# Three layers in one kernel: activations transposed in 32 x 32 squares on VectorE and through memory, side work metered by VectorE columns, float32 products in larger groups

## Chip, core and metric

The kernel runs on one core of a Trainium2 chip. The metric is device time in microseconds (us); shown are the median and the spread of three runs. The profile is of one further execution, taken by the hardware profiler. Four engines compute: TensorE (PE; its loads of stationary operands are listed apart as PEld), VectorE (DVE), ScalarE (ACT) and GpSimd (POOL). SyncE (SP), ACT and POOL can each start DMA transfers from a queue of their own.

## The reference

The input x has 4 sequences of 1024 rows with 256 channels. Three layers follow, each added to its input:

```python
def ffn(x):                      # applied to layernorm(x), times 0.5
    h = silu(x @ w1.T * s1) * (x @ w2.T * s2)     # 256 -> 1024
    h = gelu(h @ h1.T * t1)                       # 1024 -> 1024
    h = gelu(h @ h2.T * t2)                       # 1024 -> 1024
    return h @ w3.T * s3                          # 1024 -> 256
def mix(x):                      # applied to layernorm(x)
    K = kernel taps of length 1024 for each channel, from exp, sin and cos of parameters
    y = irfft(rfft(x, 2048) * rfft(K, 2048))[:1024]     # along the sequence
    return gelu(y) @ W.T + b
x = x + 0.5 * ffn(layernorm(x)); x = x + mix(layernorm(x)); x = x + 0.5 * ffn(layernorm(x))
```

The weights of `ffn` are whole numbers -1, 0 and 1, and all arithmetic has to be good to float32.

## The kernel before

**Blocks.** The 4096 rows are cut into 8 blocks of 512. The first feed-forward layer is done for blocks f0 to f7, then the last for g0 to g7, one after another by `ffn` (L275). Between them lies `mix` (L698), once for each sequence (two blocks); it needs both f blocks of its sequence and has to be stored before the first g block of that sequence is read.

**A block.** The feed-forward products have the channels on the partitions and the 512 rows as the moving columns. Activations are kept in two parts, the value rounded to a shorter float (fp32r) and what is left of it, so each product is done twice with the same weights (`linear`, L263, matmul on L267). Layer 1 makes `pa` and `pb` for eight m; layers 2 and 3 make one `p` for each of eight m, 16 matmuls each. After each `p`, ACT does the gelu (L299) and the rounding (L301), and DVE subtracts to get the low part (`low_part`, L240). At the end `result` multiplies the last activations, now the stationary side, with `w3_sb` (matmul `po`, L323), 64 matmuls; for each half of these, `finish` scales on DVE, adds the block's input on POOL and stores.

**Next block's input.** `prepare` (L834) is a generator that is advanced by `ahead()`. Before, `ahead()` is called after each of the eight m of layer 3 and once more with `last=True`. It loads the next block's 512 rows, normalises them (`norm`, L208: statistics on DVE, square root on ACT, two-operand scaling on DVE) and, at `last=True`, calls `transposed` (L242): eight TensorE transposes of 128 x 128 into two PSUM banks (L248), from which DVE makes the rounded and the low part. Rows lie on partitions as `positions` says: partition p holds rows 8p to 8p+7 of its sequence, and a block is one half of these eight.

**Side work.** `tick()` (L871) advances `all_aside` (L856) by one step, 15 times for each block: after each m of layers 2 and 3 but the last of each, and once after `ahead(last=True)`. `all_aside` first computes the kernel's taps (`kernel_steps`, L501), their transform (`kernel_spectrum`, L670), then the four `mix`. These use plain float32 matmuls: `pk` (L552), `pf` (L621), `pi` (L791), `pw` (L811). A step is what lies between two `yield`; how much DVE work is in it differs. In `kernel_steps`, each step multiplies one group of eight channels on DVE and issues the `pk` products of the group before. In `spectrum` (L593) each step issues the products of one of four q. After the 60th tick every third also runs a step of `weight_checks` (L362): a copy of the weights is read again and compared on DVE. If the side work is not far enough when a g block wants its rows, `prepare` drains it in a loop.

**Order.** The instructions of each engine are issued in one order, fixed when the kernel is built. It follows the order of the code, but a scheduler may put a later instruction ahead of one that it takes to be not ready. Small tiles of 512 columns (`half`, L132) share 19 slots, the two-part activations (`ring`, L136) 15, the 512-row inputs (`xb`) 3, and PSUM has 8 banks. All loads and stores after the start are on the queue of SP.

Of the kernel before, what the change touches and what calls it, by code (L numbers as in the profile page):

```python
# [17 lines left out]
P = 128  # L18
# [6 lines left out]
JT = TB // P  # L25
N2 = 32
# [6 lines left out]
STEPS = 2 * KH - 1  # L33
# [22 lines left out]
CST_WIDTH = 56  # L56

# [36 lines left out]
def macaron_layers(  # L94
# [32 lines left out]
    tt, ts, stt = nc.vector.tensor_tensor, nc.vector.tensor_scalar, nc.vector.scalar_tensor_tensor  # L127
# [22 lines left out]
    w3_sb = keep.tile([P, KH, D], wide, name="w3_sb")  # L150
# [8 lines left out]

    k_hat = dram.tile([2 + len(PAIRS), 2, P, 2, D], F32, name="k_hat")  # L160
# [6 lines left out]

    def load_x(t, blk, name, queue=nc.sync):
        b, g = divmod(blk, J // JT)
        xb = work.tile([P, JT, D], F32, tag="xb", name=name, bufs=3)  # L170
        queue.dma_start(xb, positions(t, b, g * JT, JT))
        return xb
# [4 lines left out]

    weights_from = nc.gpsimd if split else nc.sync

    x_first = work.tile([P, JT, D], F32, tag="xb", name="x_f0", bufs=3)  # L180
    for i, queue in ((0, nc.sync), (2, nc.scalar)):
        queue.dma_start(x_first[:, i : i + 2, :], positions(x, 0, i))
# [10 lines left out]

    x_second = load_x(x, 1, "x_f1", queue=weights_from)
# [4 lines left out]
    for t, src in ((h1_sb, h1), (h2_sb, h2)):  # L199
        for k in range(0, KH, 2):  # L200
            weights_from.dma_start(t[:, k : k + 2, :], rows(src)[:, k : k + 2, :])
    weights_from.dma_start(w3_sb, rows(w3))
# [5 lines left out]
    def norm(t, name, parts_of=1):  # L208

        stats = small.tile([P, JT, 6], F32, tag="stats", name=f"stats_{name}")  # L210
        mv = small.tile([P, JT, 2], F32, tag="mv", name=f"mv_{name}")
        rstd = small.tile([P, JT], F32, tag="rstd", name=f"rstd_{name}")
        step = JT // parts_of
        for at in range(0, JT, step):
            here = range(at, at + step)
            for i in here:
                nc.vector.bn_stats(stats[:, i, :], t[:, i, :])
            for i in here:
                nc.vector.bn_aggr(mv[:, i, :], stats[:, i, :])
            nc.scalar.activation(  # L220
                rstd[:, at : at + step], mv[:, at : at + step, 1], AF.Sqrt, bias=eps
            )
# [15 lines left out]
    def low_part(t, src):  # L238

        return tt(t[:, 1, :], src, t[:, 0, :].bitcast(F32), ALU.subtract)  # L240

    def transposed(xn, name, first=False):  # L242

# [18 lines left out]

    def linear(ps, w, m, acts):  # L263
# [11 lines left out]
    def ffn(xt, src, dst, blk, name, tick, ahead, final):  # L275

        ha = []
        for m in range(KH):  # L280
# [6 lines left out]
            stt(g if split else t[:, 0, :], pb, sc_sb[:, 1, m : m + 1], g, ALU.mult, ALU.mult)  # L287
# [4 lines left out]
        for layer, w in ((2, h1_sb), (3, h2_sb)):  # L292
            hb = []
            for m in range(KH):
# [9 lines left out]
                if layer == 3:  # L304
                    ahead()
                if m < KH - 1:
                    tick()
            ha = hb
        ahead(last=True)
        tick()  # L310
        b, g = divmod(blk, J // JT)
        rest = []
        for i in range(0, JT, 2):
            xr = half(f"xr_{name}_{i}", 2, D)
            nc.sync.dma_start(xr, positions(src, b, g * JT + i))
            rest.append(xr)
# [14 lines left out]
        def finish(ps, y, xr, i, n, add_on):  # L331
            stt(
# [8 lines left out]
            nc.sync.dma_start(positions(dst, b, g * JT + i, n), y)  # L341
# [20 lines left out]
    def weight_checks():  # L362
# [9 lines left out]
        assert len(todo) == N_CHECKS  # L372
        for n, (src, held) in enumerate(todo):
            given = half(f"given_{n}", *held.shape[1:])
            nc.sync.dma_start(given, src)
# [14 lines left out]
        nc.vector.tensor_reduce(total, miss[:, 0:N_CHECKS], axis=mybir.AxisListType.X, op=ALU.add)  # L390
        ps = psum.tile([1, 1], F32, tag="ps", name="p_bad")
# [109 lines left out]
    def kernel_steps():  # L501
# [7 lines left out]
        for g0 in range(0, DD, group):  # L509
# [34 lines left out]
            def products():  # L544

                nonlocal pk
                for d1, a in ready:
                    at = d1 % per_tile
                    if at == 0:
                        pk = psum.tile([P, per_tile, 2, NB], F32, tag="ps", name=f"pk_{g0 + d1}")  # L550
                    for i in range(n):
                        nc.tensor.matmul(  # L552
                            pk[0:NA, at + i, :, :].rearrange("p h b -> p (h b)"),
                            a[:, i].rearrange("p a b -> p (a b)"),
                            qd[d1 // per_tile][:, at + i, :, :].rearrange("p h b -> p (h b)"),
                            start=True,
                            stop=True,
                        )
                    if at + n == per_tile:
                        first = g0 + d1 + n - per_tile  # L560
                        for i, t in enumerate(taps):
                            for over in range(NB // J):
                                b0 = over * J + 2 * i
                                nc.scalar.copy(
                                    t[over * NA : (over + 1) * NA, :, :, first : first + per_tile],
                                    pk[0:NA, :, :, b0 : b0 + 2].rearrange("p d h b -> p b h d"),
                                )
                ready.clear()

            for d1 in range(0, group, n):  # L570
# [12 lines left out]
                products()  # L583
                ready.append((d1, a))
                yield
            products()
# [6 lines left out]
    def spectrum(rows_of, name, over=1):  # L593
# [39 lines left out]
        m_next = matrix(order[0])  # L633
        yield
        got = {}
        for n, q in enumerate(order):
            m = m_next
            if n + 1 < len(order):
                m_next = matrix(order[n + 1])
            products(q, m)  # L640
            if n:
                sums(order[n - 1])
            if n == 3:
                a0 = add(u[0], u[2], ALU.add, "a0")
                a1 = add(u[0], u[2], ALU.subtract, "a1")
            yield
        sums(order[3])
        b0, b1 = add(u[1], u[3], ALU.add, "b0"), add(u[1], u[3], ALU.subtract, "b1")
        yield
# [20 lines left out]
    def kernel_spectrum():  # L670
# [5 lines left out]
        for got in spectrum(rows_of, "k", over=NB // J):  # L676
            yield
        minus = half("k_minus", 2, D)
        for n, m in enumerate((0, 4)):
            t = got[m]  # L680
            nc.scalar.mul(minus[:, n, :], t[:, 1, :], -1.0)
            for e in range(2):
                nc.sync.dma_start(k_hat[n, 0, :, e], t[:, 0, :])
            nc.sync.dma_start(k_hat[n, 1, :, 0], minus[:, n, :])
            nc.sync.dma_start(k_hat[n, 1, :, 1], t[:, 1, :])
            yield
        for n, (a, b) in enumerate(PAIRS):
# [4 lines left out]
            nc.sync.dma_start(k_hat[n, 0, :, 0], t[:, 0, :])  # L692
            nc.sync.dma_start(k_hat[n, 0, :, 1], o[:, 0, :])
            nc.sync.dma_start(k_hat[n, 1, :, 0], minus[:, 0, :])
            nc.sync.dma_start(k_hat[n, 1, :, 1], t[:, 1, :])
            yield

    def mix(b):  # L698

        xn = [load_x(x1, 2 * b + g, f"xm_{b}_{g}") for g in range(2)]  # L700
        yield
        for g in range(2):
            yield from norm(xn[g], f"m{b}_{g}")
        got = None
        for got in spectrum(lambda j: xn[j // JT][:, j % JT, :], f"m{b}"):
            yield
# [17 lines left out]
        yield  # L724
# [50 lines left out]
        for j in range(JQ):  # L775
# [8 lines left out]
            if j % 2:  # L784
                yield
        banks = [[bank(f"pi_{b}_{dc}_{e}") for e in range(2)] for dc in range(DC)]
# [15 lines left out]
        yield  # L802
        for j in range(0, J, 2):
            xr = half(f"xr_{b}_{j}", 2, D)
            nc.sync.dma_start(xr, positions(x1, b, j))
            if j % 4 == 0:
                yield
            ps = bank(f"pw_{b}_{j}")
            for e in range(2):
                for dc in range(DC):  # L810
                    nc.tensor.matmul(  # L811
                        ps[:, e * D : (e + 1) * D],
                        yts[dc][j // JQ][:, (j % JQ + e) * P : (j % JQ + e + 1) * P],
                        wt_sb[:, dc, :],
                        start=(dc == 0),
                        stop=(dc == DC - 1),
                    )
            y = half(f"yw_{b}_{j}", 2, D)
            tt(
                y,  # L820
                ps.rearrange("p (e d) -> p e d", e=2),
                bias_sb[:, None, :].to_broadcast([P, 2, D]),
                ALU.add,
            )
            nc.gpsimd.tensor_tensor(y, xr, y, ALU.add)
            nc.sync.dma_start(positions(x2, b, j), y)
# [7 lines left out]
    def prepare(turn, blk, upcoming):  # L834

        name = f"{turn}{blk}"
        if turn == "f":
# [3 lines left out]
        else:  # L841
            while ("m", blk // 2) not in done:
                next(aside, None)
            xb = load_x(x2, blk, f"x_{name}")
# [5 lines left out]
        while True:  # L850
            if ("last layer", blk, turn) in done:
                upcoming.extend(transposed(xb, name))
                return
            yield

    def all_aside():  # L856
# [3 lines left out]
        yield from kernel_spectrum()  # L860
        for b in range(B):
            while ("f", 2 * b + 1) not in done:
                yield
            yield from mix(b)
# [4 lines left out]
    ticks = 0  # L869

    def tick():  # L871

        nonlocal ticks
        next(aside, None)
        ticks += 1
        if ticks > 4 * STEPS and ticks % 3 == 0:
            next(checks, None)
# [7 lines left out]
    xt, last_split = transposed(x_first, "f0", first=True)  # L885
    for n, (turn, blk) in enumerate(blocks):
# [92 lines left out]
```

## Time and profile before

| what | value |
|---|---|
| median of three runs (lowest to highest) | 1430.31 us (1430.04 to 1430.56) |
| the profiled execution: its time, its span | 1430.35 us, 1428.6 us |
| DVE busy | 835.0 us (58%) |
| ACT busy | 678.6 us (48%) |
| POOL busy | 81.6 us (6%) |
| DMA: bytes moved, mean rate | 85.50 MB, 60 GB/s |
| matmuls `p` of layers 2 and 3 | 4096, 0.39 us each by their own duration |
| transposes `pt` | 128, 0.27 to 0.29 us each by their own duration |

The span is the time from the first to the last instruction; the device time is a little longer. A matmul's own duration is longer than the distance to the next one, since matmuls are pipelined: what a matmul costs the engine is the distance between starts, not the duration. The chain of waits follows the work that ended last back to the start and gives each piece the time by which it delayed the end, which for a full TensorE comes to the same thing. A wait is listed with the engine that waited, what it waited for, the total, the count and the longest one.

### The profile page before, as it was taken

To read this page: it belongs to the slowest core of one execution; us is meant where nothing else is said; L and a number is where in the kernel's file an instruction comes from. 1 tells how busy PE (TensorE), PEld (TensorE's weight loads), DVE (VectorE), ACT (ScalarE), POOL (GpSimd) and SP (SyncE) were. 2 spreads that over 40 slices of the span, in tenths; PEclk is the share of its full clock that TensorE was granted. 3 is DMA by queue.
4 is the path that set the end of the run, shared out by engine and by line. 5 is a ranking of instruction groups with operands and counts; after the bars stand their busy time and mean duration, and the time that the engine had idled before them with its cause. 6 is when DMAs were issued, how large, how long until landed. Compare 5 with 4: busy or idle time off the path is not lost.

```text
span 1428.6 us, 18125 instructions
## 1 busy us (share of the span) xinstructions
PE 1416.6 (99%) x7092; PEld 1199.8 (84%) x7092; DVE 835.0 (58%) x1584; ACT 678.6 (48%) x1033; POOL 81.6 (6%) x82
## 2 busy tenths in 40 slices
PE   9999999999999999999999999999999999999997
PEld 7888888888888888888888888888888888888886
DVE  6786566753836577562877633867447766341412
ACT  5875468744435435344453433534345344443432
POOL 4010000100000000020000010000010000100000
PEclk9999999999999999999999999999999999999999
DMA  9010000101122140140231130231131301200000
GB/s 372 36 45 0 31 15 1 45 4 44 69 85 67 38 134 21 60 133 16 74 96 51 45 127 15 75 96 38 60 103 59 92 35 41 92 30 1 23 8 18
DMA packets 43278, 85.50 MB, mean 60 GB/s; under 512 B 4832, under 2 KB 10208, under 8 KB 43184
## 3 DMA queue, kind: packets, MB, share of 16 engines
q1 hardware_dynamic: 38016, 70.04, 15.1%
q0 software_dynamic: 5024, 13.96, 2.8%
q8 instruction: 57, 0.93, 0.3%
q14 instruction: 37, 0.30, 0.1%
q10 hardware_dynamic: 144, 0.26, 0.1%
HBM read 69.04 MB, written 15.20 MB: 59 GB/s over the span
## 4 chain that ended last, share of the span: by engine, by line
PE 97%; DVE 1%; ACT 1%; DMA 0%; issue 0%; POOL 0%; POOLq 0%
PE p_g L267 33%; PE p_f L267 31%; PE po_g L323 4%; PE pa_f L267 4%; PE pa_g L267 4%; PE pb_f L267 4%; PE pb_g L267 4%; PE po_f L323 4%; PE pi L791 2%; PE pw L811 2%; PE pf_m L621 2%; PE pk L552 1%; PE pf_k L621 0%; PE pt_f L248 0%; PE pt_g L248 0%; PE warm L882 0%
## 5 line engine op out<-in xcount | busy, mean ns | idle before, releaser
L267 PE MATMUL p_f<-h_f,h_sb 128*128 128x512 f32 x1024 | 239.1, 392 | 0.0
L267 PE MATMUL p_f<-ha_f,h_sb 128*128 128x512 f32 x1024 | 237.7, 391 | 0.0
L267 PE MATMUL p_g<-h_g,h_sb 128*128 128x512 f32 x1024 | 236.0, 390 | 0.0
L267 PE MATMUL p_g<-ha_g,h_sb 128*128 128x512 f32 x1024 | 235.0, 390 | 0.0
L267 PEld LDWEIGHTS p_f<-ha_f,h_sb 128*128 128x128 f32 x1024 | 191.5, 188 | 40.8 <-DVE ha_f L240 0.8
L267 PEld LDWEIGHTS p_g<-h_g,h_sb 128*128 128x128 f32 x1024 | 192.3, 188 | 39.8
L267 PEld LDWEIGHTS p_g<-ha_g,h_sb 128*128 128x128 f32 x1024 | 192.1, 188 | 39.7
L267 PEld LDWEIGHTS p_f<-h_f,h_sb 128*128 128x128 f32 x1024 | 191.4, 188 | 40.0 <-DVE h_f L240 0.3
L299 ACT ACTIVATE g_g<-p_g,sc_sb 128x512 f32<-128x512 f32 x128 | 88.2, 690 | 273.5 <-PE p_g L267 267.7
L240 DVE TENSOR_TENSOR h_g<-g_g,h_g 128x512 fp32r<-128x512 f32 x128 | 88.3, 692 | 221.7 <-ACT h_g L301 221.7
L240 DVE TENSOR_TENSOR h_f<-g_f,h_f 128x512 fp32r<-128x512 f32 x128 | 88.4, 691 | 190.1 <-ACT h_f L301 189.9
L299 ACT ACTIVATE g_f<-p_f,sc_sb 128x512 f32<-128x512 f32 x128 | 88.1, 689 | 220.2 <-PE p_f L267 211.4
L301 ACT CAST h_g<-g_g 128x512 fp32r<-128x512 f32 x128 | 79.3, 620 | 3.9
L301 ACT CAST h_f<-g_f 128x512 fp32r<-128x512 f32 x128 | 79.0, 618 | 3.2
L267 PE MATMUL pa_f<-xt_f,w_sb 128*128 128x512 f32 x256 | 69.7, 391 | 0.7 <-DVE xt_f L254 0.7
L267 PE MATMUL pb_f<-xt_f,w_sb 128*128 128x512 f32 x256 | 69.1, 389 | 0.0
L267 PE MATMUL pa_g<-xt_g,w_sb 128*128 128x512 f32 x256 | 68.6, 390 | 0.0
L267 PE MATMUL pb_g<-xt_g,w_sb 128*128 128x512 f32 x256 | 68.4, 389 | 0.0
L286 ACT ACTIVATE g_g<-pa_g,sc_sb 128x512 f32<-128x512 f32 x64 | 43.4, 689 | 52.6 <-PE pa_g L267 49.7
L323 PE MATMUL po_f<-w_sb,h_f 128*128 128x256 f32 x512 | 64.4, 285 | 1.3 <-ACT h_f L301 1.0
L323 PEld LDWEIGHTS po_f<-w_sb,h_f 128*128 128x128 f32 x512 | 62.4, 192 | 2.0 <-ACT h_f L301 1.2
L323 PE MATMUL po_g<-w_sb,h_g 128*128 128x256 f32 x512 | 63.7, 285 | 0.0
(230 smaller groups left out, 1636.0 us busy)
## 6 DMA issues: line engine op xcount, KB each, us to landing
h_sb<-in_h_dram POOLq DMA_DIRECT2D x8, 1024.0 KB, 13.9
given<-in_h_dram SPq DMA_DIRECT2D x32, 256.0 KB, 3.1
kr<-k_hat SPq DMA_DIRECT2D x20, 256.0 KB, 2.6
ki<-k_hat SPq DMA_DIRECT2D x20, 256.0 KB, 2.9
xr_f<-in_x_dram SPq DMA_DIRECT2D x16, 256.0 KB, 4.2
x<-y_f SPq DMA_DIRECT2D x16, 256.0 KB, 2.4
xm<-x SPq DMA_DIRECT2D x8, 512.0 KB, 4.7
m_m<-in_cosm_dram SPq DMA_DIRECT2D x16, 256.0 KB, 4.2
```

The source lines that it names most:

```text
L240: return tt(t[:, 1, :], src, t[:, 0, :].bitcast(F32), ALU.subtract)
L267: nc.tensor.matmul(ps, w[:, k, m * P : (m + 1) * P], acts[k][:, part, :], start=(k == 0 and part == 0), stop=(k == n - 1 and part == parts ...
L286: nc.scalar.activation(g, pa, AF.Silu, scale=sc_sb[:, 0, m : m + 1])
L299: nc.scalar.activation(g, ps, AF.Gelu, scale=sc_sb[:, layer, m : m + 1])
L301: nc.scalar.copy(t[:, 0, :], g)
L323: nc.tensor.matmul(ps[:, e * D : (e + 1) * D], ha[k][:, part, (i + e) * P : (i + e + 1) * P], w3_sb[:, k, :], start=(k == 0 and part == 0) ...
L552: nc.tensor.matmul(pk[0:NA, at + i, :, :].rearrange("p h b -> p (h b)"), a[:, i].rearrange("p a b -> p (a b)"), qd[d1 // per_tile][:, at + ...
L621: nc.tensor.matmul(ps[e][:, part, :], m[:, e, part, :], rows_of(q + JQ * e), start=True, stop=True)
L791: nc.tensor.matmul(banks[dc][e][:, q * P : (q + 1) * P], vs[q + JQ * e][:, part, dc * P : (dc + 1) * P], m[:, e, part, :], start=(part == ...
L811: nc.tensor.matmul(ps[:, e * D : (e + 1) * D], yts[dc][j // JQ][:, (j % JQ + e) * P : (j % JQ + e + 1) * P], wt_sb[:, dc, :], start=(dc == 0),
```

## The change

Eleven of the fifteen blocks that are prepared ahead (f1 to f7, and g1, g3, g5, g7) no longer go through `transposed`. Their rows are loaded in four DMAs, each onto 32 partitions, so that a transpose of 32 x 32 squares on DVE (`squares`) leaves pieces that eight stores and two loads through a buffer in memory (`moved`) put into place. `parted` then makes the two parts from SBUF. The four others (g0, g2, g4, g6) keep TensorE's transposes and now start their load nine calls later. `ahead()` is called in layer 2 too, so 16 times and the last, and the steps of a block are spread over these. Blocks hold consecutive rows (`tokens`) instead of `positions`.

`tick()` is called after every m of layer 2 and all but the last of layer 3, and no more after `ahead(last=True)`. It counts DVE work (columns plus 130 for each operation) and takes steps until 2500 are done since the last tick, or until a step yields `PAUSE`; weight checks run from g0 on, in ticks that a pause leaves with room. `prepare`'s own DVE work counts too.

`pk` products are issued two groups at a time, `pf` for two q at a time, `pw` for two j at a time. Stores of intermediate results move from the queue of SP to that of POOL; `x_second` is loaded after the weights of layers 2 and 3; `w3_sb` is moved by 40 words within a tile that is 128 words wider.

```diff
+STEP_WORK, OP_WORK, MIN_WORK = 2500, 130, 300
+W3_APART, W3_BEHIND = 40, 88
...
+    w3_at = keep.tile([P, W3_APART + KH * D + W3_BEHIND], wide, name="w3_sb")
+    w3_sb = w3_at[:, W3_APART : W3_APART + KH * D].rearrange("p (k d) -> p k d", k=KH)
...
+    stores = nc.gpsimd
...
     def load_x(t, blk, name, queue=nc.sync):
...
-        queue.dma_start(xb, positions(t, b, g * JT, JT))
+        src = t[b, g * TB : (g + 1) * TB, :].rearrange("(j s a) d -> a s j d", s=SQ, a=JT)
+        for a in range(JT):
+            queue.dma_start(xb[a * SQ : (a + 1) * SQ], src[a])
...
+    def squares(xn, name):
+        out = []
+        for k in range(DC):
+            sq = half(f"sq_{name}_{k}", P // SQ, JT, SQ)
+            squares_of(
+                sq, xn[:, :, k * P : (k + 1) * P].rearrange("p j (c r) -> p c j r", r=SQ)
+            )
+            for a in range(JT):
+                stores.dma_start(
+                    moved[k].rearrange("(c r) a q -> a r c q", r=SQ)[a],
+                    sq[a * SQ : (a + 1) * SQ].rearrange("r c j s -> r c (j s)"),
+                )
+            yield
+        yield
+        for k in range(DC):
+            t = half(f"xf_{name}_{k}")
+            stores.dma_start(t, moved[k].rearrange("d a q -> d (a q)"))
+            out.append(t)
+        yield out
+
+    def parted(xf, name):
+        xt = []
+        for k, src in enumerate(xf):
+            t = ring(f"xt_{name}_{k}", parts, TB, dtype=wide)
+            nc.vector.tensor_copy(t[:, 0, :], src)
+            if split:
+                low_part(t, src)
+            xt.append(t)
+        return xt
...
-                if layer == 3:
-                    ahead()
-                if m < KH - 1:
+                ahead()
+                if layer == 2 or m < KH - 1:
                     tick()
             ha = hb
         ahead(last=True)
-        tick()
...
                 tt(a, a, o, ALU.add)
-                products()
                 ready.append((d1, a))
+                if len(ready) == 4:
+                    for old in ready[0:2]:
+                        products(*old)
+                    del ready[0:2]
                 yield
-            products()
+            yield PAUSE
+            for old in ready:
+                products(*old)
             yield
...
+        by_squares = turn == "f" or blk % 2 == 1
...
+            if not by_squares:
+                for _ in range(9):
+                    yield
             while ("m", blk // 2) not in done:
                 next(aside, None)
-            xb = load_x(x2, blk, f"x_{name}")
+            xb = (load_x if by_squares else load_rows)(x2, blk, f"x_{name}")
+        yield
         yield
         yield
         for _ in norm(xb, name):
             yield
             yield
-        while True:
-            if ("last layer", blk, turn) in done:
-                upcoming.extend(transposed(xb, name))
-                return
+        if by_squares:
+            for xf in squares(xb, name):
+                yield
+        while ("last layer", blk, turn) not in done:
             yield
+        upcoming.extend(parted(xf, name) if by_squares else transposed(xb, name))
...
     def tick():
-        nonlocal ticks
-        next(aside, None)
+        nonlocal ticks, allowed, work_done
         ticks += 1
-        if ticks > 4 * STEPS and ticks % 3 == 0:
-            next(checks, None)
+        allowed = min(allowed, work_done) + STEP_WORK
+        while work_done < allowed:
+            at = work_done
+            if next(aside, PAUSE) is PAUSE:
+                if len(done) > 8 and allowed - work_done > OP_WORK + TB:
+                    next(checks, None)
+                break
+            if work_done == at:
+                work_done += MIN_WORK
```

## Prediction

> **What bounds the kernel now.** First the page's busy shares and slices, then its chain of waits.
>
> ```profile
> PE 1416.6 (99%) x7092; PEld 1199.8 (84%) x7092; DVE 835.0 (58%) x1584; ACT 678.6 (48%) x1033; POOL 81.6 (6%) x82
> PEclk9999999999999999999999999999999999999999
> PE 97%; DVE 1%; ACT 1%; DMA 0%; issue 0%; POOL 0%; POOLq 0%
> ```
>
> TensorE never has a free slice, its clock is full and 97% of the chain is its own work. Its matmuls start at 2.6 us and end at 1421.1. So only two things count: what leaves or joins TensorE's queue, and where TensorE comes to stand. A busy share can't show the price of a piece, because pipelined matmuls overlap; the chain can. The end of one block, the chain between 430 and 440 us:
>
> ```profile
> 429.82 5.90 PE p_f L267 x26
> 435.72 0.87 PE pt_f L248 x8
> 436.59 3.47 PE po_f L323 x29
> ```
>
> The eight transposes of the next block stand between layer 3 and the output products: 0.87 us. Starts within them are 109 ns apart. Now the float32 tap products, the chain between 140 and 160 us, and TensorE's list of waits for its weight loads:
>
> ```profile
> 144.36 3.85 PE p_f L267 x16
> 148.22 1.05 PE pk L552 x16
> 149.26 3.85 PE p_f L267 x16
> ```
>
> ```profile
> PEld pk L552 <- issue: 5.5, 16, 0.4
> ```
>
> Sixteen `p` elsewhere take 3.64 us (16 times 227 ns), here 3.85: each of the 16 groups of `pk` costs 1.05 + 0.21 = 1.26 us, though its own matmuls start 58 ns apart (16 x 58 = 0.93). The rest, 0.34, is paid at the turn into and out of the group; the list has it as 5.5/16. The other float32 groups pay no such turn: eight `pf` take 1.73 us, which is 8 times their distance of 216 ns.
>
> **The change, part by part.**
>
> *Transposes off TensorE.* Eleven blocks times 0.87 = **-9.57 us**. Here a rule would mislead. The row of `pt` says 272 to 287 ns each, and the Trainium skill (TensorE: Matmul & The Clock Gate, "Part 4: PE-mode transpose") gives some 275 ns in a kernel. By that, 88 x 275 ns = 24.2 us would go and the kernel would fall to 1406. Rule and row agree on the duration, but the distance between starts is 109 ns; I take 0.87 a block.
>
> *What those 0.87 us covered.* After the last `p` of layer 3, ACT does gelu and rounding and DVE the low part, and the 16th `po` needs it, 15 x 0.12 = 1.80 us after the first. With the transposes ahead it is needed at 2.67. One block has no transposes ahead of `po`, the last; its timeline:
>
> ```profile
> 1413.25 0.69 ACT L299 ACTIVATE g_g<-p_g,sc_sb 128x512 f32<-128x512 f32 x1 [2.29 <-PE p_g L267]
> 1413.97 0.62 ACT L301 CAST h_g<-g_g 128x512 fp32r<-128x512 f32 x1
> 1414.63 0.69 DVE L240 TENSOR_TENSOR h_g<-g_g,h_g 128x512 fp32r<-128x512 f32 x1 [2.94 <-ACT h_g L301]
> 1415.37 5.57 PEld L323 LDWEIGHTS po_g<-w_sb,h_g 128*128 128x128 f32 x46 [0.19 <-DVE h_g L240]
> ```
>
> The low part ends 2.11 us after the last `p` (1413.21), 0.3 late; the chain gives this `po` 7.94 us where others have 7.67. So every block that loses its transposes gains a stall of at least 0.27: 11 x 0.27 = 3.0. That is with DVE idle. The new copies of `parted` need no TensorE, so they may run on DVE just then; one 512-column operation (0.69) in front of each low part makes it 11 x 0.96 = 10.6. At six of the eight block ends that I looked at the low part starts within 0.04 us of ACT's rounding, so I take the low end plus two ends with 1.0 more: **+5.0**; both ends go into the range.
>
> *Stalls that exist now.* 1.11 us in f0's `po` (at 86 us, behind three ACT table loads of 1.28 each) and 0.39 in f7's (710 us, behind side work on DVE). Both places change, and such ends are in the two above: **-1.5**. The start (8 us until full speed) and the end (7.4 us after the last matmul) stay.
>
> *Larger groups.* 16 `pk` groups become 8, if the steps come as in the code: 8 x 0.34 = **-2.7**; 0 if the scheduler splits each pair. `pf`, `pw` and `pi` pay no turn: nothing. Pairing holds four PSUM banks until DVE has added the first two results. If the second pair of `pf` must wait for that, DVE is 2.5 us (to the low part) and two additions of 0.69 behind `p`, TensorE three products of 0.86: 1.3 us in each of five transforms, 6.7 in all. I take 0, since the order was made so that no `pf` waits now, and keep 6.7 for the range.
>
> *Work added elsewhere.* DVE: 22 transposes of 512 columns, for which there is no row; the fastest 512-column row is 0.43, the slowest 0.88, I take 0.69: 15 us, on 835. The 22 copies take 0.43 to 0.69 where the casts from PSUM took 0.69. All beside TensorE. DMA: per block four loads in place of one, eight stores and two loads. They are issued on POOL at 0.55 to 0.73 us each (rows of its issues), 110 in all; with the 52 stores moved there from SP some 100 us more on POOL's 82. Squares are made at calls 8 and 9 of `ahead`, fetched at call 11 and used after call 17. From call 9 that is eight `p` of 3.63, 29 us, against 0.7 for the square, 3.3 for six issues, and landings of some 2.7 and 4: 11 us. Covered by 18. SP gains three issues a load and loses the stores behind which its loads stood (it waited 139, 78 and 72 us for POOL's sums). Against POOL speaks the same skill (SBUF — State Buffer, "SBUF: two separate sides"): a DMA issued from GpSimd can't get its descriptors written while DVE holds the shared port in a two-port operation, 620 ns alone against 3100. By the row the ten issues of a block are 6 us of POOL, by the rule up to 31, more than the 29 at hand. The only rows so fast that they point to such a mode, plain scaling of 512 columns in 0.43 us, are few and short, so I take the row.
>
> *Metering.* A tick is 2500 units; 512 columns count 642 and take 0.685 us, so a tick is 2.67 us of DVE, with the low part 3.36 against 3.63 of TensorE. It fits, with an overshoot of at most one step. Counted from the code: taps and transform 130 thousand units, a `mix` 63 thousand with 11 pauses, `prepare` 5.9 thousand a block against 37.5 thousand of ticks. The fourth `mix` then ends in g5's layer 3 by a short drain, where it ends now (its `pw` at 1219 us). So **0**.
>
> *The move of w3.* `po` matmuls start 120 ns apart, while half of `pf`'s 216 for the same 256 columns (two records for each of its matmuls) would be 108. If the place matters, 1024 x 12 ns = 12 us go; against it, 227 and 120 hold everywhere, whatever tile is read. I take 0.
>
> **Sum**: 1428.6 - 9.6 + 5.0 - 1.5 - 2.7 = 1419.8 of span; the median lies 1.7 above this span: **1421.5 us**.
>
> **Rivals.**
>
> - *The cover is needed at every end* (10.6 instead of 5.0, or splits of `pk` and waits of `pf`): 1427 to 1431. For: no slack at the last block's `po`, DVE at 60 to 75% in most blocks. Against: the scheduler may issue other `po` first.
> - *Squares come late* (the slower side). The copies wait in DVE's in-order queue for the fetch, and low parts, gelu banks and `po` stand behind. Cause: the 19 slots. A `mix` holds 12 to 16 of them, `squares` adds four; SP already waits 67 us for one. The margin is 18 us; every us beyond it costs 11. From 1.1 us a block on the gain of 12.3 is gone; at 2 us, 1430 - 12 + 22 - 1 = 1439. For: slots are full now. Against: the scheduler sees slots and defers other work.
> - *w3's place matters*: 1421.5 - 12 = 1410.
> - *Groups don't form*, since the scheduler takes another order: 1424.
>
> **Chances.** The forecast with its own spread (1416 to 1427, the split groups in it) 0.61; cover needed everywhere 0.16, a third of it still faster; late squares or starved side work 0.15; w3 0.08. A change under 0.2% (2.9 us) can't be told from none. Faster: 0.61 + 0.08 + 0.05 = 0.74; same 0.11; slower 0.15. The range leaves out half of w3's case and most of the slower one: 1412 to 1433.
>
> **What would show it.** `pt` down to 40 matmuls; pieces of 32 `pk` at 2.2 us; `po` pieces of 7.9 to 8.3 after f1 to f7 squares and odd g, released by DVE's low part; no `pf` piece over 3.5 us for 16. If `po` waits for DVE with a copy of `xt` in front, the first rival holds; if DVE waits for a DMA of `xf` there, squares are late; if `po` starts 108 ns apart, w3's place counts. A POOL queue whose issues take 3 us would void the row taken for it.

## The result, and the profile after

| | before | changed |
|---|---|---|
| median of the runs side by side | 1430.43 us (4 runs) | 1417.82 us (4 runs, 1417.21 to 1418.74) |
| ratio | | 0.9911, 95% interval 0.9893 to 0.9928 |
| profiled execution: span, first `p` at, last matmul ends | 1428.6, 23.8, 1421.1 us | 1416.8, 25.5, 1409.9 us |

The change saves 12.6 us; 8.9 were forecast (1421.5). The new profiled execution is the slowest of its four runs (1418.74), because of its first microseconds, as will be seen. Its page, first the busy shares, then the granted clock in 40 slices, then the chain by engine:

```profile
PE 1404.9 (99%) x7004; PEld 1190.3 (84%) x7004; DVE 841.1 (59%) x1606; ACT 687.0 (48%) x1039; POOL 182.6 (13%) x267
PEclk9999999999999999999999999999999999999999
PE 94%; ACT 4%; DVE 1%; issue 0%; DMA 0%; DVEq 0%; ACTq 0%
```

TensorE still sets the end: 88 matmuls fewer (7092 to 7004), and the span is shorter by about what left its queue. New is ACT's 4% of the chain: it stands ahead of the ends of f0 (60 to 88 us) and f2 (214 to 258 us), of which more below. POOL is up by 101 us, as its 185 more instructions suggest, and TensorE waits for it only at the start (2.6 us, as before). The chain where f1 ends (start, duration, what):

```profile
147.01 1.98 PE pk L640 x32
148.99 3.85 PE p_f L348 x16
152.84 1.98 PE pk L640 x32
...
171.76 7.82 PE po_f L402 x64
```

Two groups of `pk` now go in one turn: 1.98 + 0.21 = 2.2 us for 32 matmuls, where two turns of 16 took 2.5. Ahead of `po` no `pt` stands. The same place where it works best, the end of f4:

```profile
424.93 13.60 PE p_f L348 x60
438.53 7.60 PE po_f L402 x64
```

No transposes and no wait. TensorE's list of waits for its weight loads (total us, times, longest), first of `po` before, then changed:

```profile
PEld po_f L323 <- ACT h_f L301: 1.2, 1, 1.2
PEld po_f L323 <- DVE h_f L240: 0.5, 1, 0.5
```

```profile
PEld pk L640 <- issue: 2.8, 8, 0.4
...
PEld po_f L402 <- DVE h_f L286: 1.4, 4, 0.9
...
PEld po_f L402 <- ACT h_f L383: 0.8, 1, 0.8
PEld po_g L402 <- DVE h_g L286: 0.6, 3, 0.2
```

`pk` has halved (5.5 us, 16 times before); `po` now waits in more places, but little in each. The work that took the transposes' place, as groups by line (busy us, mean ns of one, then idle time ahead and its cause):

```profile
L141 DVE STREAM_TRANSPOSE sq_f<-x_f 128x512 f32<-128x512 f32 x14 | 9.9, 705 | 0.0
L338 DVE CAST xt_f<-xf_f 128x512 fp32r<-128x512 f32 x14 | 5.5, 420 | 0.0
L321 POOL DMA_DIRECT2D moved<-sq_f x56 | 30.8, 558 | 196.3 <-DVE sq_f L141 196.3
L329 POOL DMA_DIRECT2D xf_f<-moved x14 | 7.8, 560 | 19.1 <-DMA moved<-sq_f 15.0 <-ACT a_b L497 2.1 <-DVE stats_m L141 2.0
```

DVE stood idle for 0.0 us ahead of the copies of `xt`: it never waited for a fetch, so the squares are in time.

The starts of all matmuls, taken group by group in both traces, give this account (us, changed less before; the forecast's +5.0 and -1.5 stand in one row, since f0's wait belongs to both):

| | forecast | measured |
|---|---|---|
| `pt`: 11 blocks less | -9.6 | -9.57 (11 x 0.87) |
| `pk`: 8 turns less | -2.7 | -2.69 (16 x 1.269 to 8 x 2.203) |
| `po` waits, 16 block ends | +5.0 - 1.5 | +1.7 (2.20 to 3.89) |
| distance of `po` starts, 1024 | 0 | -1.6 (119.9 to 118.3 ns) |
| short waits of `p` elsewhere, `pf`, `pw`, `pi` | 0 | about -0.7 (what is left) |
| up to the first `p` | 0 | +1.7 in this one execution |
| last matmul to the end | 0 | -0.5 (7.43 to 6.90) |

The +1.7 belongs to this execution and not to the change: its granted clock was half for the first products of the first block. A slice of the page is 35 us, too long to show that; a stretch of its own does (from:to, its length, busy us and count of PE, PEld, DVE, ACT and POOL, then the granted clock, the DMA share and GB/s), the changed kernel first, then the one before:

```profile
9.30:12.70 3.40, 3.40 (x8) 2.73 (x9) 1.60 (x3) 1.20 (x1) 1.48 (x3) 0.50 1.13 423
```

```profile
9.30:12.70 3.40, 3.40 (x15) 2.55 (x14) 0.94 (x2) 1.63 (x3) 1.36 (x2) 1.00 1.09 409
```

The matmuls there start 427 ns apart in place of 227. Four profiled executions have such a stretch (this one and, of those below, w3 taken back, all squares and metering off): their first `p` comes at 25.5 to 25.8 us, that of the ten others at 23.8 to 24.9, and three of the four were the slowest of their runs. What lowers the clock here is not shown: TensorE was busy for 2.08 us between 6 and 9 us here, and for 1.86 in an execution (matrices moved by 160 bytes) whose clock stayed full.

### The profile page after: what moved, and what is told of

Its sections match the earlier page's. It is cut to its first block, busy times and chain, and to the rows that moved or that the text cites. A ratio compares the mean times of both kernels' runs of the same rounds, so it can differ in the third digit from the quotient of the medians.

```text
span 1416.8 us, 18331 instructions
## 1 busy us (share of the span) xinstructions
PE 1404.9 (99%) x7004; PEld 1190.3 (84%) x7004; DVE 841.1 (59%) x1606; ACT 687.0 (48%) x1039; POOL 182.6 (13%) x267
## 4 chain that ended last, share of the span: by engine, by line
PE 94%; ACT 4%; DVE 1%; issue 0%; DMA 0%; DVEq 0%; ACTq 0%
PE p_g L348 33%; PE p_f L348 28%; PE po_g L402 4%; PE pa_f L348 4%; PE pb_f L348 4%; PE pa_g L348 4%; PE pb_g L348 4%; PE po_f L402 4%; PE pi L891 2%; PE pw L916 2%; PE pf_m L713 2%; PE pk L640 1%; ACT L381 1%; ACT g_f L381 1%; ACT h_f L383 1%; PE pf_k L713 0%
## 5 line engine op out<-in xcount | busy, mean ns | idle before, releaser
L366 ACT ACTIVATE g_f<-pa_f,sc_sb 128x512 f32<-128x512 f32 x64 | 43.8, 687 | 53.6 <-PE pa_f L348 51.3
L419 POOL TENSOR_TENSOR y_g<-xr_g,y_g 128x512 f32<-128x512 f32 x15 | 19.3, 1286 | 380.0 <-DVE y_g L411 350.6
```

The costliest lines, as they stand in the source:

```text
L366: nc.scalar.activation(g, pa, AF.Silu, scale=sc_sb[:, 0, m : m + 1])
L419: add_on.tensor_tensor(y, xr, y, ALU.add)
```

## The experiments

**One part alone, on the kernel before.** Only the place of w3:

```diff
-    w3_sb = keep.tile([P, KH, D], wide, name="w3_sb")
+    w3_at = keep.tile([P, 40 + KH * D + 88], wide, name="w3_sb")
+    w3_sb = w3_at[:, 40 : 40 + KH * D].rearrange("p (k d) -> p k d", k=KH)
```

> The kernel before with one edit: w3_sb moved by 40 words in a tile that is 128 words wider. If its place sets the pace of the output products, their starts go from 120 ns apart to 117 to 119, as in the changed kernel, and 1024 of them give 1 to 3 us: 1428 to 1429. If the pace came with the changed order of work, starts stay at 120 and the time at 1430.4.

Measured: 1429.01 us against 1430.23, ratio 0.9991 (0.9984 to 0.9998), -1.2 us; its output products start as close as in the changed kernel (118.4 ns, 118.3 there). Only the pairs of `pk` (two groups held back, then issued together):

```diff
-                products()
+                if len(ready) == 3:
+                    late = ready[2:]
+                    del ready[2:]
+                    products()
+                    ready.extend(late)
                 ready.append((d1, a))
```

> The kernel before with one edit: the tap products are issued two groups at a time. If the turn into and out of a group is what costs, 8 groups of 2.20 us replace 16 of 1.27: 2.7 us less, 1427.7. If the pairing pays only together with metering (the scheduler splits the pairs, or TensorE waits for VectorE's factors), 1429.5 to 1431.

Measured: 1427.44 us, ratio 0.9979 (0.9970 to 0.9988), -2.8 us. The price of a turn, 0.34 us, holds.

**The place of w3 taken back** in the changed kernel (`W3_APART, W3_BEHIND = 0, 128`):

> The changed kernel with w3_sb back at its old place (the tile stays 128 words wider). Place theory: output products at 120 ns again and 1 to 3 us more than 1417.8, so 1419 to 1421. Order theory: 1417.8.

Measured: 1419.16 us (1418.93 to 1420.92), +1.3. The same block end, f4, in the chain of this run:

```profile
439.38 7.67 PE po_f L402 x64
```

7.67 against 7.60 for 64 products. Both directions agree on 1.2 to 1.3 us.

**All transposes back on TensorE,** in the changed kernel, twice. First with each block's rows in one load again:

```diff
-        by_squares = turn == "f" or blk % 2 == 1
+        by_squares = False
...
-            xb = x_second if blk == 1 else load_x(x, blk, f"x_{name}", queue)
+            xb = x_second if blk == 1 else load_rows(x, blk, f"x_{name}")
```

> The changed kernel with all fifteen blocks transposed on TensorE again (rows loaded in one DMA); metering, grouping, stores and w3 stay. If the transposes are the gain: eleven times 0.87 us come back, 9.6, and the stalls of the eleven ends (3.6 in the profile) mostly go: 1423 to 1425. If metering and the freed queues are the larger part: under 1421.

Measured: 1435.61 us, ratio 1.0042 (1.0028 to 1.0056): slower than the kernel before, and 17.8 above the changed one. The expectation missed by 11 us. Then with f1's rows left on POOL's queue, since that had also been moved:

> The changed kernel with all transposes back on TensorE, as in the earlier run that came out at 1435.6, but the second block's rows keep the changed kernel's queue and place in it. Theory: the eleven transposes are worth 0.87 each and the waits that they cover at the block ends come off (1.8 us of 0.28 each): 1417.8 + 9.6 - 1.6 = 1425 to 1427 us, if the 10 us more of the earlier run were its wait in f0 behind ACT's table loads and the longer tail after the last matmul. Rival: those belong to the transposes being on TensorE (or to GpSimd's queue being empty) and return: 1432 to 1437 us.

Measured: 1434.48 us, ratio 1.0031 (1.0019 to 1.0043). The rival holds: the excess comes back. Against the changed kernel's trace the span grew by 16.4: eleven more groups of `pt` take 9.6 (15 groups in all after the first, 13.08 us), the waits of `po` at the other 15 ends shrink by 2.1 (0.76 in place of 2.83), the wait at the end of f0 grows by 4.8, and the time from the last matmul to the end grows by 3.8 (10.74 against 6.90). The start of this execution is 0.9 shorter, since its clock was full there, so that 1.2 us are still to be placed: 0.7 lie in three of the next block's first products, which stand among these `po`; 0.5 stay open. The list of waits names the first of the two additions:

```profile
PEld po_f L403 <- ACT h_f L384: 3.9, 3, 1.9
```

and the timeline shows ACT there:

```profile
84.72 0.69 ACT L382 ACTIVATE g_f<-p_f,sc_sb 128x512 f32<-128x512 f32 x1
85.42 1.28 ACT L498 ACT_TABLE_LOAD   x1
86.72 0.63 ACT L498 ACTIVATE a_b<-a_b 128x512 f32<-128x512 f32 x1
...
88.50 1.28 ACT L382 ACT_TABLE_LOAD   x1
89.79 0.69 ACT L382 ACTIVATE g_f<-p_f,sc_sb 128x512 f32<-128x512 f32 x1
90.51 0.62 ACT L384 CAST h_f<-g_f 128x512 fp32r<-128x512 f32 x1
...
91.18 0.50 PEld L403 LDWEIGHTS po_f<-w_sb,h_f 128*128 128x128 f32 x2 [1.94 <-ACT h_f L384]
```

Between two gelus stands a function of the side work (L498), and each change of function costs a table load of 1.28 us. Gelu and rounding of the last tile end at 91.1, some 8 us behind the last `p` (4 in the changed kernel). ACT has no room there. Layer 3 of f0 as one stretch, in this run, in the changed kernel and in the run without metering (below):

```profile
53.60:82.50 28.90, 28.90 (x129) 23.77 (x128) 22.63 (x51) 28.50 (x34) 0.00 (x0) 1.00 0.00 1
```

```profile
54.50:83.60 29.10, 29.10 (x129) 23.80 (x128) 27.12 (x70) 26.39 (x33) 7.11 (x13) 1.00 0.29 86
```

```profile
54.70:83.40 28.70, 28.70 (x128) 23.79 (x127) 16.10 (x50) 16.30 (x23) 7.09 (x13) 1.00 0.29 88
```

ACT is busy for 99%, 91% and 57% of the stretch (87% in the kernel before), with 12, 11 and 4 table loads. So more side work stands in f0 without the squares; that the meter, which counts the squares' columns too, let it in is likely, but argued, not shown. Part of the 4.8 is the clock, which is half behind the wait:

```profile
89.40:96.00 6.60, 4.87 (x20) 4.53 (x20) 5.28 (x11) 2.97 (x4) 0.00 (x0) 0.50 0.00 0
```

The longer tail is an instruction of POOL that the profile doesn't count as busy: in the trace its closing drain takes 6.9 and 7.0 us in these two runs, 1.04 in the changed kernel. So the transposes by themselves are worth 7.5 us, net of the waits that come off with them (9.6 - 2.1, and half of the 2.1 is f2's wait, which is ACT's); the rest of the 16.7 is f0's wait, its half clock and the longer drain, which came along when the squares left the side work and POOL's queue. The stores moved to POOL's queue and the later load of `x_second` were not tried alone.

**The waits of `po`.** Term 7 of each first half is put behind terms 0 to 6 of both banks:

```diff
+        result(ps0, 0, 2, [(0, early)])
+        result(ps2, 2, 2, [(0, early)])
+        result(ps0, 0, 2, [(0, late), (1, range(KH))])
...
+        result(ps2, 2, 2, [(0, late)])
+        result(ps2, 2, 2, [(1, range(KH))])
```

> The changed kernel with one alteration in the output products: the first halves of both banks run their terms 0 to 6 ahead of term 7 of either, so the low part of the eighth layer-3 tile is needed some 14 x 118 ns = 1.65 us later. My theory: what is left of the squares' price is this one wait (in the changed kernel's trace 3.9 us over 16 block ends, 2.1 of it behind table loads of ACT in f0 and f2), so nearly all of it goes: 1414 to 1415 us against 1417.8. Rival: the waits are only where the time shows, and TensorE would wait elsewhere for the same ACT and DVE work, in the next block's first banks: 1417 to 1418 us.

Measured: 1417.48 us (1417.31 to 1417.70), -0.3: the number the rival gave, but not for its reason. All waits of 0.28 are gone, at every end but those of f0 (1.06) and f2 (0.98), 2.03 us left of 3.89, and TensorE waits nowhere else instead. Of the 1.85, 1.2 were given back at the very end: the last block's first bank is complete some 1.7 us later (14 products of the second bank stand ahead), its sum on POOL and its store follow, and the span ends 8.06 us after the last matmul in place of 6.90. The rest is in the distance of the products (118.6 ns for 118.3). The waits of f0 and f2 stayed as they were; here is f0 in the changed kernel itself:

```profile
79.99 1.28 ACT L381 ACT_TABLE_LOAD   x1
81.29 0.69 ACT L381 ACTIVATE g_f<-p_f,sc_sb 128x512 f32<-128x512 f32 x1
82.00 1.28 ACT L577 ACT_TABLE_LOAD   x1
83.29 0.63 ACT L577 ACTIVATE e_b<-e_b 128x512 f32<-128x512 f32 x1
...
84.45 1.28 ACT L381 ACT_TABLE_LOAD   x1
85.75 1.26 ACT L381 ACTIVATE g_f<-p_f,sc_sb 128x512 f32<-128x512 f32 x2
86.90 1.14 ACT L383 CAST h_f<-g_f 128x512 fp32r<-128x512 f32 x2
...
87.55 1.29 DVE L286 TENSOR_TENSOR h_f<-g_f,h_f 128x512 fp32r<-128x512 f32 x2 [1.21 <-ACT h_f L383]
87.57 0.30 PEld L402 LDWEIGHTS po_f<-w_sb,h_f 128*128 128x128 f32 x2 [0.76 <-ACT h_f L383]
```

ACT is a whole tile behind, with three table loads in this stretch: the gelus of the seventh and the eighth tile follow each other at 85.75, 2 us after the last `p` has started. TensorE's long wait, before its 25th `po`, ends with the first of the two roundings. It is for the seventh tile, term 6, and the edit moved only term 7. So these two waits show nothing against the reordering.

**The last four blocks by squares too** (`by_squares = True`, loads from the predecessor's first calls of `ahead` on):

> The changed kernel with the last four blocks that TensorE still transposes (g0, g2, g4, g6) turned by squares too, their rows loaded early in the predecessor. By the step of the prediction (0.87 us a block go, up to 0.28 come back as a wait of the output products): -3.5 + 1.1 at most, 1415.4 to 1414.3 us. Rival, squares late: these four have their rows from the mix that ends in the predecessor's first half; if the fetch lands late, the copies hold DVE and the time is 1418 us or more.

Measured: 1415.82 us (1415.36 to 1417.21), ratio 0.9897 (0.9882 to 0.9912), -2.0. The waits of `po` grew by 1.2 us to 5.1, nearly all of it in pieces of 0.28, so of 4 x 0.87 = 3.5 us 2.3 are left; 0.5 of that goes into a longer end (7.36 us after the last matmul in place of 6.90). Squares were not late.

**Metering off.** Each tick issues one step:

```diff
-STEP_WORK, OP_WORK, MIN_WORK = 2500, 130, 300
+STEP_WORK, OP_WORK, MIN_WORK = 1, 130, 300
```

> The changed kernel with the metering off: each tick issues one step of the side work, whatever DVE columns it holds. The prediction priced the metering at 0: 1417 to 1419 us. Rival: without it the side work comes late (its pauses each take a tick now), the rest of each mix is drained in one piece in front of a g block's rows, DVE's queue holds the low parts back and the squares of odd g come late: 1422 to 1440 us, with waits of p or po for DVE's low part.

Measured: 1722.34 us, ratio 1.2038, some 280 us above the highest that was expected. Slices and waits:

```profile
PE   9999999999999953343999919999199993799990
PEclk9999999999999975576999959999699996899995
```

```profile
PEld pi L891 <- issue: 155.9, 4, 39.0
PEld pk L640 <- issue: 73.5, 3, 41.5
PEld p_bad L481 <- DVE total L478: 34.4, 1, 34.4
PEld pf_m L713 <- issue: 12.3, 1, 12.3
```

TensorE stands still where the rest of the tap products, the transforms and the checks are drained in one piece, with nothing of the blocks beside them. These waits add up to 276 of the 305 us. The granted clock is half in these stretches (0.50 from 627 to 736 us, and four times for some 40 us later), and the matmuls issued there start at twice their distance: some 23 us, an estimate from their starts. The steps and pauses of the changed kernel can only be afforded with the meter; what a meter would do for the steps of the kernel before was not tried. The run also answers the question of f0: with little side work in it, that end looks like this:

```profile
83.87 0.69 ACT L381 ACTIVATE g_f<-p_f,sc_sb 128x512 f32<-128x512 f32 x1 [2.29 <-PE p_f L348]
84.59 0.62 ACT L383 CAST h_f<-g_f 128x512 fp32r<-128x512 f32 x1
...
85.99 5.46 PEld L402 LDWEIGHTS po_f<-w_sb,h_f 128*128 128x128 f32 x46 [0.19 <-DVE h_f L286]
```

The same 0.28 (0.19 of it at the weight load) as the last block has had all along: gelu starts at once, and there is no table load between it and the rounding.

**Places in SBUF.** The gain of w3 asked for more. By their sizes, all matrices and activations of the kernel before stand at the same place within 512 bytes; the changed kernel puts w3 160 bytes off the others. First everything behind w3 was moved by 160 bytes (`W3_BEHIND = 128`), activations among it:

> The changed kernel with everything that lies behind w3 in SBUF moved by another 160 bytes (unused columns), so that activations, w3 and the 512-column moving operands of layers 1 to 3 stand at the same place within 512 bytes, and w1, w2, h1, h2 as before. Theory A, the place of w3 relative to the stationary operand counts: output products go back to 120 ns, +1.3 us, and the 5120 matmuls of layers 1 to 3, whose two operands now stand apart, may come 1 to 2 ns nearer each, -5 to -10 us: 1408 to 1414. Theory B, the place of the moving operand by itself: output products stay at 118.3, the others gain: 1407 to 1413. Theory C, only w3's own place, or a 256-column matter: 1417 to 1419, and layers 1 to 3 stay at 227 ns.

Measured: 1454.62 us, +36.8. None of the three. Then the four matrices of layers 1 to 3 alone, by 160 and by 256 bytes (unused columns ahead of w1):

> The changed kernel with w1, w2, h1 and h2 also moved by 160 bytes in SBUF (unused columns ahead of them); w3 and the activations stand where the change put them. In the run with everything behind w3 moved, the matmuls of layers 1 to 3 went from 227 to some 234 ns with weights at 0 and activations at 160 bytes, and the output products back from 118.3 to 119.8. Theory A, the difference of the two operands' places counts: apart again, so layers 1 to 3 slow down as there, 1440 to 1460 us. Theory B, the moving operand's own place counts (activations back at 0): 227 ns and 1416 to 1419 us. Theory C, the place of matrices counts and 160 bytes is good for them as for w3 (-1.6 ns of each): 1408 to 1413 us.

> The changed kernel with w1, w2, h1 and h2 moved by 256 bytes in SBUF in place of 160; w3 and the activations where the change put them. With the two operands of layers 1 to 3 160 bytes apart (in either sense) their matmuls came 231 to 235 ns after each other in place of 227. Theory A, any distance within 512 bytes costs: 1430 to 1455 us. Theory B, it is the 160 bytes, which are no multiple of 64: 227 ns again, 1416.5 to 1419 us.

Measured: 1449.03 us (+31.2) and 1417.40 us (1417.27 to 1418.04, no difference). Layer 3 near 430 us in the chain, of the first, second and third of these runs:

```profile
428.64 18.74 PE p_f L348 x80
447.37 7.68 PE po_f L402 x64
```

```profile
427.39 18.66 PE p_f L349 x80
446.05 7.59 PE po_f L403 x64
```

```profile
424.89 12.47 PE p_f L349 x55
```

That is 234, 233 and 227 ns for a matmul of 512 columns. With activations or matrices 160 bytes off, each of the 5120 costs some 7.5 or 6.5 ns more, 38 or 33 us in all, of which shorter waits of `po` (2.1 and 2.4 us in place of 3.9) give back over 1; 256 bytes cost nothing. The output products lose their gain (7.68) when activations stand at 160 bytes like w3. What makes 160 good for one and bad for the other, and whether it is the distance of the two operands, was not settled: no run had matrices and activations both at 160.

**All that helped, together:** all squares; term 7 late, except in the last block; and no tick in layer 3 of f0 and f2 from the sixth tile on:

```diff
-                if layer == 2 or m < KH - 1:
+                if layer == 2 or m < (5 if name in ("f0", "f2") else KH - 1):
                     tick()
```

> The changed kernel with: all squares (that run gave 1415.8); term 7 of both first halves late, in all blocks but the last (in its own run the waits of 0.28 went, 1.85 us in all, but the tail after the last matmul grew by 1.2 since the first bank ended later); and no tick in layer 3 of f0 and f2 from the sixth tile on, so that no table load of ACT stands behind the last gelus there (2.1 us of waits). Theory: 1415.8 - 2.9 - 1.9 = 1411 to 1412 us. Rival: the table loads only move to another end, or the side work that is put off by six ticks is drained later: 1413 to 1416 us.

Measured: 1412.25 us (1411.98 to 1412.35), ratio to the kernel before 0.9875 (0.9860 to 0.9890): 5.6 us under the changed kernel, the fastest of all. Waits of `po` come to 0.38 us over 16 ends, 0.10 in f0, none in f2, 0.28 in the last. What each of the three parts gave here can't be told apart, but ACT has 124 table loads in all in this fastest kernel and 110 in the changed one: it is not their number that counts. This end of f4 has neither transposes nor a wait:

```profile
428.28 3.64 PE p_f L348 x16
431.92 7.60 PE po_f L402 x64
```

## Why the prediction was right, and where it was off

*Transposes, 11 x 0.87.* Right. The distance of starts was the price, not the duration, and the 24.2 us that the duration would have taken off never appeared. (The 275 ns of the Trainium skill, TensorE: Matmul & The Clock Gate, "Part 4: PE-mode transpose", belong to transposes in bfloat16 and these are float32; that the two agree says little.) The fifteen groups in the run with TensorE's transposes cost 0.87 each again.

*What they covered, +5.0 and -1.5.* Right in kind, too large in size: net +1.7 for +3.5, which is 3.6 of waits that are there now, the last block's left out, and 1.9 that went. The low end, 0.27, was the right price of an end (0.28 in the trace), but two of the eleven ends that lost their transposes, f4 and f5, pay nothing and three others 0.04 to 0.19. The order issued explains it: at every such end products of the second bank stand ahead of the one that needs the last low part, three of them at f1, f3, g2 and g6 (0.28 each), four at g0 (0.16), five at g4 (0.04), more at f4 and f5. The prediction had that only as a word against its first rival. The rival's sign itself, a copy of `xt` in front of the low part on DVE, shows in the wait of one end, f6: there the low part starts 0.4 us behind the rounding, and with seven products ahead 0.19 is left. Two ends with waits of about 1.0 exist, f0 and f2, but that the guess of two came out is luck. It is not DVE with a copy in front but ACT with table loads, and f0 had its wait before, too. The run without metering and the last run, which take the side work out of these ends, bring f0 from 1.06 to 0.28 and 0.10.

*Larger groups, -2.7.* Right: -2.69 in the trace, -2.8 alone. No pair of `pf` waited; all cost 3.46 us, twice 1.73. (The 6.7 kept for the range is 6.5 by its own terms, five times 1.3.)

*Work elsewhere at nothing.* Right. The DVE transpose measured 0.705 (0.69 taken), POOL's issues 0.55 to 0.57 us. The rule weighed against it (the Trainium skill, SBUF — State Buffer, "SBUF: two separate sides"), by which a DMA from POOL can take 3100 ns beside a two-port operation of DVE, shows in no row here: the longest of POOL's 206 issues took 0.90 us. It was hardly put to the test, since only 15 of them overlap one of DVE's operations of some 0.4 us.

*Metering at 0.* The sum against before is small, as forecast, but the step hid two things. The changed kernel's steps need the meter: without it 300 us are lost. And its unit is DVE's column, so a step with a table load of ACT (1.28 us) counts as little as any other. Where several loads fall into the last tiles of a block, TensorE pays: 2.1 us in the changed kernel, at f0 and f2 (1.2 before, at f0 alone). Their number does not decide: it is 104 before, 110 changed and 100 in the form with TensorE's transposes (f1's rows on POOL's queue). In that form f0 alone loses 5.9: 4.1 us of waits and 1.8 of matmuls at half clock behind them.

*Place of w3 at 0.* Off by 1.2 to 1.6 us: the place does count, in the direction of the rival, at an eighth of the rival's 12. "227 and 120 hold everywhere, whatever tile is read" was true of the kernel before, but there all matrices and activations stand at the same place within 512 bytes: its profile could not show what a place costs that no tile had.

*Start and end "stay".* The end is 0.5 shorter; the start is 1.7 longer in the profiled execution, by the half clock, which comes and goes from one execution to the next.

So the forecast lay 3.7 us high: 1.8 from the waits' size, about 1.4 from w3, the rest from the short waits and the end. These misses add up, none hides another. Of the rivals, "squares come late" and "groups don't form" did not occur; "cover needed at every end" paid 0.28 at some ends and was cured by reordering.

## What to carry to other kernels

When a small piece leaves a saturated TensorE, price it by the distance of its starts, then ask what work of other engines it gave time to; the cheapest repair of the new wait is to put products that don't need the late operand in front of the one that does, in every block but the last, where it delays the final store. A meter for side work must count what the side work costs on every engine that the main chain passes through; here one that counts DVE's columns alone let ACT's table loads pile up around the gelus that TensorE waits for. And moving a tile for other reasons can move the pace of every matmul that reads it: compare the distance of starts before and after, not only the instructions.

## What the runs showed of the hardware that was not expected

- The place of an operand in SBUF counts for the pace of float32-rounded matmuls: 227 ns for 512 columns with both operands at the same place within 512 bytes or 256 bytes apart, 233 to 234 (single ones 230 to 238) with one of them 160 bytes off; 120 ns for 256 columns with both at the same place, 118.3 with the moving operand 160 bytes off, 119.8 with both moved by 160.
- POOL's closing drain took 1.04 us in the seven profiled kernels that issue 206 DMAs on POOL, 4.31 in the two with 246, 6.9 and 7.0 in those with 84 and 85, and 1.78 in three of the form before, with 21. The longest pushed the end of the span out by 3.8 us; what sets it was not tried.
- The granted clock fell to half for 3.4 us at the start of four of the fourteen profiled executions, for 3.4 and 6.8 us behind the long wait of f0 in the two with TensorE's transposes, and for up to 109 us in the run without metering, where TensorE mostly stood still; matmuls then started at twice their distance (427 ns in place of 227). Shorter waits of TensorE, up to 1.2 us at one block end, left the clock full. Except for that last run the page's 40 slices show none of it.
